# A windowed attention of a vision block on one core: per-query products and sums, and the same attention as matmuls over pairs of key rows

## The chip, the core and the metric

The kernel runs on one core of a Trainium2 chip. Five engines run their own queues of instructions and meet through semaphores: TensorE (PE in the profile; PEld are its weight loads), VectorE (DVE), ScalarE (ACT), GpSimd (POOL) and SyncE (SP), which here issues all DMAs. The metric is the device time of one execution in microseconds; lower is better.

## What is computed

The reference is a stack of layers on x of shape (2, 256, 56, 56) in float32. The change touches the first two of them, here cut to what matters. Group normalisation comes first, with groups of 8 channels; then attention over 7x7 windows with 8 heads of 32 channels, **without a softmax**; then a projection; then a position term from five values per pixel is added. `unfold` lists the 49 neighbours of each of the L = 50 x 50 window places; `attn_idx` gives every one of the 56 x 56 queries its window (the edge queries share the outermost ones).

```python
qkv = einsum('oc,bchw->bohw', qkv_w, x) + qkv_b
q = q * hd ** -0.5
def unfold(t):
    p = conv_general_dilated_patches(t, (7, 7), (1, 1), 'VALID')
    return p.reshape(B, C, L, 49)
k_u = unfold(k).reshape(B, nh, hd, L, 49).transpose(0, 1, 3, 2, 4)
k_g, v_g = k_u[:, :, attn_idx], v_u[:, :, attn_idx]
attn = einsum('bnld,bnldk->bnlk', qh, k_g) + bias
out = einsum('bnlk,bnlkd->bnld', attn, v_g)
x = x + einsum('oc,bchw->bohw', proj_w, out) + proj_b
```

The patches come out with the 49 taps ahead of the places, and `reshape(B, C, L, 49)` reads them as places ahead of taps. So the 49 keys of window place n are the elements 49 n to 49 n + 48 of the list "tap by tap, all places of a tap": nearly always a run of one tap over neighbouring pixels, that is pieces of one or two rows of the image. The rest of the reference (six state-space layers, a gated feed-forward layer, a causal attention, a mixture of eight experts) isn't touched.

## The kernel before

Three phases run one after the other: `conv_phase` (these two layers; it stores its result t1 to DRAM), `mamba_phase` and `tail_phase`. The order of instructions on each engine is the order of the Python calls; semaphores are set by the tile framework from the buffers that are read and written.

In `conv_phase` the 56 x 56 pixels are 7 chunks of 448 (CT). The channels are 2 x 128 partitions. `normalise` (L167 to L196) takes statistics with BatchNorm instructions (L172), sums them over the groups with a matmul (L177, L186), and scales x (L194). `project` (L199) makes q, k and v (L206 matmul, L216 ACT copy), kept as qo, kt, vt with channels on partitions.

The attention runs in 672 slots of 10, 10 or 8 queries: per image, 56 query rows of two halves of three slots each. For each half of a window row, `gather` (L294, copy L309 on ACT) puts the keys that the queries see into a row kr in the order of the queries, 49 per query, and the values likewise into vr; `edges` (L314, POOL) repeats the outermost window for the three edge queries. Then, slot by slot:

- `products` (L330, POOL, L335): key times query, elementwise, 128 partitions x 2 x 490;
- `sums` (L342, PE): the bias comes in as a matmul of a one-hot table with the bias table (L360), then a matmul with a block matrix of ones adds the 32 channels of a head and spreads the sum back to them (L368), both as 64x64 tiles at four positions of the array;
- `values` (L374, DVE): the score times the value, elementwise from PSUM (L377), and a sum over each 49 (L380), into qo.

The main loop (L443 on) calls products(i + 2), sums(i + 1), one step of `side_work` and values(i). `side_work` (L399) is a generator: the rest of the projections, the position term (`position`, L144; it goes to DRAM as pe_d, since the reference reads it with another shape), the second image's load and normalisation, and `output` (L228): it loads x and pe_d for a chunk (L231, L233), adds them on POOL (L236), multiplies by the projection (L244), adds on DVE (L253) and stores t1 (L261). Lines L461 on belong to mamba_phase: its first instructions are L487 (DVE), L490 (SP), L722 (SP, the load of t1's first chunk) and L727 (PE).

Of the kernel before, what the change touches and what calls it, by code (L numbers as in the profile page):

```python
# [18 lines left out]
P = 128  # L19
B = 2  # L20
# [9 lines left out]
OQ = 10  # L30
# [29 lines left out]

@with_exitstack
def conv_phase(ctx: ExitStack, tc: tile.TileContext, I, t1_d):


# [11 lines left out]
    HR = 25  # L76
    EDGE = 3 * KK
    HALF = HR * LW + EDGE
# [4 lines left out]
    rowp = ctx.enter_context(tc.tile_pool(name="cv_row", bufs=2))  # L83
    wp = ctx.enter_context(tc.tile_pool(name="cv_work", bufs=2))
    pmm = ctx.enter_context(tc.tile_pool(name="cv_pmm", bufs=2, space=PSUM))
    patt = ctx.enter_context(tc.tile_pool(name="cv_patt", bufs=3, space=PSUM))
# [7 lines left out]
    xg = big.tile([P, 2, S], F32, name="xg")  # L94
    kt = big.tile([P, 2, HW, HW], F32, name="kt")
    vt = big.tile([P, 2, HW, HW], F32, name="vt")
    qo = big.tile([P, 2, S], F32, name="qo")

    def load(b):
        for k in range(2):  # L100
            nc.sync.dma_start(xg[:, k, :], x_v[b, :, k, :])

    load(0)
    gmat = cp.tile([P, P], F32, name="gmat")
    nc.sync.dma_start(gmat, I["gmat"])
    wqkv = cp.tile([P, 2, 3 * C], F32, name="wqkv")
    nc.sync.dma_start(wqkv, I["qkv_wT"].rearrange("(k p) o -> p k o", p=P))
# [3 lines left out]
    rb = cp.tile([P, WS * 3 * 4], F32, name="rb")  # L111
    nc.sync.dma_start(rb, I["rel"])
    onehot = cp.tile([P, 3 * OQ * KK + 2 * (OQ - 2) * KK], F32, name="onehot")
    nc.sync.dma_start(onehot, I["onehot"])
    hmat = cp.tile([P, 2 * HD], F32, name="hmat")
    nc.sync.dma_start(hmat, I["hmat"])
    wproj = cp.tile([P, 2, C], F32, name="wproj")
    nc.sync.dma_start(wproj, I["proj_wT"].rearrange("(k p) o -> p k o", p=P))
    pew = cp.tile([5, C], F32, name="pew")
    nc.sync.dma_start(pew, I["pe_w"])  # L120
    eps = ones_column(nc, cp, 1e-5, "gn_eps")

    rel = cp.tile([P, WS, 3, 2, 2 * HD], F32, name="rel")
    nc.gpsimd.tensor_copy(
        rel.rearrange("j i c f (m d) -> j (i c f m) d", d=HD),
        rb.unsqueeze(2).to_broadcast([P, WS * 3 * 4, HD]),
    )

# [4 lines left out]
    def flow(groups):  # L133

        last = None
        for first, second in groups:
            first()
            if last:
                last()
            last = second  # L140
            yield
        last()

    def position(q):  # L144
        pos = wp.tile([5, CT], F32, name="pos", bufs=1)
        nc.sync.dma_start(pos, I["pos"][:, chunk(q, CT)])
        yield

        def group(i):
            pp = []  # L150

            def first():
                pp.append(mm())
                nc.tensor.matmul(
                    pp[0][:TK, :C], lhsT=pos[:, chunk(i, TK)], rhs=pew, start=True, stop=True
                )

            def second():
                pe = wp.tile([TK, C], F32, name="pe")
                nc.scalar.copy(pe, pp[0][:TK, :C])  # L160
                nc.sync.dma_start(pe_d[chunk(q * (CT // TK) + i, TK), :], pe)

            return first, second

        yield from flow(group(i) for i in range(CT // TK))

    def normalise():  # L167

        for k in range(2):
            st = wp.tile([P, NC, 6], F32, name="st")  # L170
            for j in range(NC):
                nc.vector.bn_stats(st[:, j, :], xg[:, k, chunk(j, CT)])  # L172
                yield
            mv = wp.tile([P, 2], F32, name="mv")
            nc.vector.bn_aggr(mv, st)
            pg = mm()
            nc.tensor.matmul(pg[:, 0:1], lhsT=gmat, rhs=mv[:, 0:1], start=True, stop=True)  # L177
            yield
            gm = wp.tile([P, 1], F32, name="gm")
            nc.vector.tensor_copy(gm, pg[:, 0:1])  # L180
            dm = wp.tile([P, 1], F32, name="dm")
            nc.vector.tensor_tensor(dm, mv[:, 0:1], gm, ALU.subtract)
            dv = wp.tile([P, 1], F32, name="dv")
            nc.vector.scalar_tensor_tensor(dv, dm, dm, mv[:, 1:2], ALU.mult, ALU.add)
            pv = mm()
            nc.tensor.matmul(pv[:, 0:1], lhsT=gmat, rhs=dv, start=True, stop=True)  # L186
            yield
            rs = wp.tile([P, 1], F32, name="rs")
            nc.scalar.activation(rs, pv[:, 0:1], AF.Sqrt, bias=eps)
            yield  # L190
            nc.vector.reciprocal(rs, rs)
            for j in range(NC):
                part = xg[:, k, chunk(j, CT)]
                nc.vector.tensor_scalar(part, part, gm, rs, ALU.subtract, ALU.mult)  # L194
                yield

    ready = set()

    def project(b, i, j, f):  # L199

        pq = []

        def first():
            pq.append(mm())
            for k in range(2):
                nc.tensor.matmul(  # L206
                    pq[0][:, :CT],
                    lhsT=wqkv[:, k, chunk(2 * i + f, P)],
                    rhs=xg[:, k, chunk(j, CT)],
                    start=(k == 0),  # L210
                    stop=(k == 1),
                )

        def second():
            dst = (qo, kt.rearrange("p f h w -> p f (h w)"), vt.rearrange("p f h w -> p f (h w)"))[i]
            nc.scalar.activation(  # L216
                dst[:, f, chunk(j, CT)], pq[0][:, :CT], AF.Identity,
                bias=vec[:, 2 * i + f : 2 * i + f + 1],
                scale=scale if i == 0 else 1.0,
            )  # L220
            ready.add((b, i, j, f))

        return first, second

    def parts(b, i, js):
        return [project(b, i, j, f) for j in js for f in range(2)]

    def output(b, j):  # L228

        xo = wp.tile([P, 2, CT], F32, name="xo", bufs=1)  # L230
        nc.sync.dma_start(xo, x_v[b, :, :, chunk(j, CT)])  # L231
        pe = wp.tile([P, 2, CT], F32, name="pe_in", bufs=1)
        nc.sync.dma_start(pe, pe_v[:, :, chunk(j, CT)])  # L233
        yield
        yield
        nc.gpsimd.tensor_tensor(xo, xo, pe, ALU.add)  # L236

        def group(f):
            po = []

            def first():
                po.append(mm())
                for k in range(2):
                    nc.tensor.matmul(  # L244
                        po[0][:, :CT],
                        lhsT=wproj[:, k, chunk(f, P)],
                        rhs=qo[:, k, chunk(j, CT)],
                        start=(k == 0),
                        stop=(k == 1),
                    )  # L250

            def second():
                nc.vector.scalar_tensor_tensor(  # L253
                    xo[:, f, :], po[0][:, :CT], vec[:, 6 + f : 7 + f], xo[:, f, :],
                    ALU.add, ALU.add,
                )

            return first, second

        yield from flow(group(f) for f in range(2))  # L260
        nc.sync.dma_start(t1_v[b, :, :, chunk(j, CT)], xo)  # L261

    halves, slots = [], []
    firsts = {}
    for b in range(B):
        for lh in range(LW):
            rows = [h for h in range(HW) if min(max(h - 3, 0), LW - 1) == lh]
            for e in range(2):  # L270
                n = len(halves)
                halves.append((b, lh, e, rows, len(slots)))
                for h in rows:
                    for w0, nq in ((0, OQ), (OQ, OQ), (2 * OQ, 8)):
                        slots.append((n, h, 28 * e + w0, nq))
        firsts[b + 1] = len(slots)
    ns = len(slots)
    K, V, PR, PA = {}, {}, {}, {}

    def pieces(n):

        b, lh, e, rows, _ = halves[n]
        a, z = (HR - 1) * e, (HR - 1) * e + HR
        found = []
        if a < lh:
            found.append((a, min(z, lh), *divmod(lh - 1, WS), LW - lh))
        if z > lh:  # L290
            found.append((max(a, lh), z, *divmod(lh, WS), -lh))
        return a, [(r0, r1, dw, dh + off) for r0, r1, dh, dw, off in found]

    def gather(n, which):  # L294
        if n >= len(halves):
            return
        b, lh, e, rows, _ = halves[n]
        a, found = pieces(n)
        for r0, r1, dw, of in found:
            for j in range((r0 + of) // CR, (r1 + of - 1) // CR + 1):  # L300
                for f in range(2):
                    while (b, 1 + which, j, f) not in ready:
                        next(work)
        t = rowp.tile([P, 2, HALF], F32, name=("kr", "vr")[which])
        (K, V)[which][n] = t
        at = 0 if e else EDGE
        m = t[:, :, at : at + HR * LW].rearrange("p f (r w) -> p f r w", w=LW)
# [1202 lines left out]
```

## Time and profile before

| what | us |
|---|---|
| runs of this kernel | 10,890.83, 10,893.99, 10,902.05 |
| their median | 10,893.99 |
| span of the profiled execution (its whole time is not listed beside it) | 10,877.0 |
| conv_phase, from the timeline: start to L261's last store | 0 to 1,668 |
| mamba_phase and tail_phase | 1,668 to 10,877 |
| busy over the span: PE / DVE / ACT / POOL | 8,985.9 / 9,661.4 / 7,670.7 / 8,265.3 |

How to read it: PE's busy time counts pipelined instructions, so 83% of the span is not PE at its peak. A row such as "L380 DVE TENSOR_REDUCE qo<-av 128x20 f32<-128x980 f32 x442 | 519.0, 1174 | 18.3 <-DVE av" says: line 380, on DVE, writes qo from av, 442 times, 519.0 us busy, 1,174 ns for one, and 18.3 us of idle time on the engine just before. The share over the whole span mixes three phases with different limits; for a change in the first one the stretches up to 1,668 us count.

### The profile page before, as it was taken

Reading aid. Unit: us, or ns where it says so; the run is one execution under the profiler, and the core shown is the slowest. Engines: PE = TensorE matmul, PEld = TensorE weight load, DVE = VectorE, ACT = ScalarE, POOL = GpSimd, SP = SyncE. Lnnn points to the kernel's source line nnn. Section 1 sums busy time; section 2 is a strip of 40 time slices with the busy share of each in tenths; the row PEclk is TensorE's granted clock in tenths of the full one; section 3 lists DMA queues with packets and bytes.
Section 4 is the critical chain, followed back from the end, with each engine's and each line's share of the span. In section 5 each row is a group of like instructions: output and inputs, shape, how many; then the busy total and the mean of one; then the engine's idle time right before and its main releaser. Section 6 shows DMA issues by size and latency. Waiting matters only on the chain. (4 is left out here: it accounts for less than half of the span.)

```text
span 10877.0 us, 121750 instructions
## 1 busy us (share of the span) xinstructions
PE 8985.9 (83%) x39394; PEld 3570.3 (33%) x39394; DVE 9661.4 (89%) x7545; ACT 7670.7 (71%) x15776; POOL 8265.3 (76%) x5268
## 2 busy tenths in 40 slices
PE   8999997777777777777777777777777777789999
PEld 3333333323322222222332222222222222245555
DVE  6998996999999999999999999999999999967453
ACT  4664665787777878778787777878787787733343
POOL 5887995788888888888888888888888888811100
PEclk9999998888888888888888888888888888799999
DMA  1000004555555555555555555555555555511111
GB/s 49 17 16 11 13 15 97 121 127 124 117 129 120 128 123 129 123 123 129 135 139 123 129 123 123 129 123 129 123 127 124 122 126 120 121 51 31 43 37 40
DMA packets 674228, 1068.88 MB, mean 98 GB/s; under 512 B 83082, under 2 KB 668050, under 8 KB 672722
## 3 DMA queue, kind: packets, MB, share of 16 engines
q1 hardware_dynamic: 673586, 1061.09, 42.0%
q8 instruction: 309, 5.06, 0.2%
q14 instruction: 333, 2.73, 0.1%
HBM read 875.91 MB, written 184.91 MB: 98 GB/s over the span
## 5 line engine op out<-in xcount | busy, mean ns | idle before, releaser
L824 POOL TENSOR_TENSOR x<-dtur,bc 128x896 f32<-128x896 f32 x2688 | 4701.9, 1771 | 109.8 <-PE acc L859 100.8
L807 ACT ACTIVATE da<-dtr,am 128x449 f32<-128x449 f32 x5376 | 3428.5, 638 | 187.8 <-DVE x L844 95.9
L844 DVE TENSOR_TENSOR_SCAN da<-da,x 128x898 f32<-128x898 f32 x1680 | 3397.5, 2022 | 150.2 <-ACT state L833 73.0
L837 POOL TENSOR_TENSOR x<-x,bc 128x896 f32<-128x896 f32 x1008 | 1788.5, 1774 | 513.3 <-ACT state L833 512.0
L562 PE MATMUL mm<-xn,w_in 128*128 128x448 f32 x2656 | 1481.2, 690 | 703.2 <-ACT hz L603 233.7
L844 DVE TENSOR_TENSOR_SCAN x<-da,x 128x898 f32<-128x898 f32 x1008 | 2002.3, 2013 | 0.7 <-ACT da L807 0.7
L837 DVE TENSOR_TENSOR x<-da,bc 128x896 f32<-128x896 f32 x1680 | 1834.5, 1092 | 82.4 <-DVE da L844 1.8
L859 PE MATMUL acc<-x,sum_w 128*32 128x448 f32 x10752 | 1565.5, 658 | 23.2 <-POOL x L837 17.3
L335 POOL TENSOR_TENSOR pr<-kr,qo 128x980 f32<-128x980 f32 (+1 forms) x672 | 1149.0, 1722 | 195.7 <-PE pa L368 185.5
L580 PE MATMUL mm<-u,w_cv 128*128 128x448 f32 x2656 | 1089.1, 553 | 175.3 <-ACT u L574 158.6
L562 PEld LDWEIGHTS mm<-xn,w_in 128*128 128x128 f32 x2656 | 549.8, 230 | 1675.2 <-issue 729.9
L833 ACT COPY state<-da 128x2 f32<-128x2 f32 x1680 | 264.0, 157 | 1058.3 <-DVE x L837 1043.6
L360 PE MATMUL pa<-onehot,rel 49*64 49x490 f32 (+5 forms) x7168 | 835.5, 558 | 111.9 <-DVE av L377 109.2
L377 DVE TENSOR_TENSOR av<-pa,vr 128x980 f32<-128x980 f32 (+1 forms) x672 | 740.2, 1102 | 113.3 <-PE pa L368 83.8
L380 DVE TENSOR_REDUCE qo<-av 128x20 f32<-128x980 f32 (+1 forms) x672 | 743.3, 1106 | 41.4 <-DVE av L377 1.0
L309 ACT COPY vr<-vt 128x2500 f32<-128x2500 f32 (+14 forms) x296 | 468.6, 1614 | 422.8 <-DVE av L377 422.5
L580 PEld LDWEIGHTS mm<-u,w_cv 128*128 128x128 f32 x2656 | 478.2, 190 | 800.0 <-issue 371.8
L652 POOL TENSOR_TENSOR dtu<-dt,hz 128x448 f32<-128x448 f32 x336 | 328.6, 978 | 450.8 <-ACT state L833 391.9
L368 PE MATMUL pa<-pr,hmat 64*64 64x490 f32 (+1 forms) x5376 | 643.4, 548 | 0.0
L708 PE MATMUL mm<-hz,w_out 128*128 128x448 f32 x1344 | 551.7, 554 | 79.5 <-DVE res L715 47.9
L633 PE MATMUL mm<-xd,w_dt 16*128 16x448 f32 x664 | 457.3, 777 | 189.9 <-ACT xd L620 110.9
L859 PEld LDWEIGHTS acc<-x,sum_w 128*32 128x32 f32 x10752 | 230.5, 117 | 1000.6 <-issue 790.4
(209 smaller groups left out, 11097.9 us busy)
## 6 DMA issues: line engine op xcount, KB each, us to landing
dtr<-dt_d SPq DMA_DIRECT2D x1344, 224.0 KB
dtur<-dtu_d SPq DMA_DIRECT2D x1344, 224.0 KB
bc<-bc_d SPq DMA_DIRECT2D x336, 448.0 KB
dt_d<-dt SPq DMA_DIRECT2D x336, 224.0 KB
dtu_d<-dtu SPq DMA_DIRECT2D x336, 224.0 KB
cb<-comb_d SPq DMA_DIRECT2D x128, 196.0 KB
t<-t_d SPq DMA_DIRECT2D x28, 448.0 KB
w_in<-in_in_w SPq DMA_DIRECT2D x12, 1024.0 KB
```

What stands on the lines that cost most here:

```text
L335: nc.gpsimd.tensor_tensor(pr[:, :, :m].rearrange("p f (q k) -> p f q k", k=KK), K[n][:, :, at : at + m].rearrange("p f (q k) -> p f q k", ...
L360: nc.tensor.matmul(pa[chunk(f, 64), g, :m], lhsT=rel[64 * g : 64 * g + rows, bh, kind, f, :], rhs=onehot[64 * g : 64 * g + rows, col : col ...
L368: nc.tensor.matmul(pa[chunk(f, 64), g, :m], lhsT=hmat[chunk(g, 64), :], rhs=pr[chunk(g, 64), f, :m], start=False, stop=True, tile_position ...
L377: nc.vector.tensor_tensor(av[:, :, :m], PA.pop(i)[:, :, :m], V[n][:, :, at : at + m], ALU.mult)
L380: nc.vector.tensor_reduce(qo[:, :, h * HW + w : h * HW + w + nq], av[:, :, :m].rearrange("p f (q k) -> p f q k", k=KK), AX.X, ALU.add,)
L562: nc.tensor.matmul(ps, lhsT=layer_of(j + 1)["w_in"][:, k, chunk(at, P)], rhs=Q["xn"][:, k, :], start=(k == 0), stop=(k == 1),)
L580: nc.tensor.matmul(ps, lhsT=layer_of(j + 1)["w_cv"][:, 4 * d + k, :], rhs=M["u", d][:, k : k + T], start=(k == 0), stop=(k == 3),)
L807: nc.scalar.activation(D[i][:, chunk(g, T + 1)], dtr[:, 2 * pr + g, :], AF.Exp, scale=L["am"][:, col : col + 1],)
L824: nc.gpsimd.tensor_tensor(x[:, :, 1:], Q[k][1][:, 2 * pr : 2 * pr + 2, :], wide(Q["bc"][:, ng, :]), ALU.mult)
L837: engine.tensor_tensor(both(X[i])[:, :, 1:], both(h)[:, :, 1:], wide(QS[j]["bc"][:, 4 + ng, :]), ALU.mult)
L844: nc.vector.tensor_tensor_scan(h, D[i], X[i], 0.0, ALU.mult, ALU.add)
L859: nc.tensor.matmul(acc[0][chunk(g, HD), :T], lhsT=sum_w, rhs=both(X[i - 1 + g // 2])[:, g % 2, 1:], start=False, stop=(ng == 3), tile_posi ...
```

## The change

`conv_phase` is written anew; only the loads of its inputs and `project`, `position`, `normalise` and `output` stay in kind. `mamba_phase` and `tail_phase` keep their code (their line numbers fall by 8).

The kernel now takes **two neighbouring rows of keys** (t - 1 and t, 112 pixels, KT) as one tile, for t = 0 to 55, and multiplies them with all the queries that use them. `key_plan` finds, at build time, for every query the tile in which its 49 keys lie, and a column s of that tile's 72 (QS). There are 48 queries whose keys are in two tiles; they get a second column and their two results are added. Everything of the attention is then matmuls with 112 keys on one side:

- `spread` copies the queries from image order (qn) into tile order (sk, 128 x 2 x 56 x 72, zero elsewhere), run by run, alternately on DVE and POOL (L274); `collect` copies the results back the same way, and adds the second columns on POOL (L297). Per image key_plan gives 228 runs and 48 second columns.
- `scores` (PE), for 7 tiles of one group and two heads: one matmul writes the bias of the inner queries (L356; a Toeplitz table `rel`, selected by a one-hot table); 14 small matmuls of key rows and queries add the scores (L365). The two heads are row tiles at different positions of the array.
- `weigh`: DVE multiplies with a mask (L375), which keeps of the 112 keys those that the query sees; POOL adds the bias of the 22 edge columns (L379).
- `value_part` (PE, L343): the values of the next group, pixels on partitions, straight from x; DVE adds their bias (L347).
- `apply` (PE, L391): 14 small matmuls of values and weighted scores; the two heads are column tiles. Every second call ACT copies the result back into sk (L398).
- `fetch` (L324 to L328) loads one-hot, mask and edge tables of the next group, 1.04 MB.

A unit is (group n, f, p): 8 groups, 4 head pairs, so 32 units per image; the order of calls is that of `attend`. Projections of all queries and keys, spread, collect and output are no longer beside the attention but before and after it; the second image's load and normalisation stay beside the first image's attention. `normalise` treats both channel halves together, `position` runs at the very start with pos lying in qn, and the x load is in smaller pieces. The tables are built on the host from the inputs, in another form than before (`layout`).

```diff
-OQ = 10
+QI = HW - 6
+QS = HW + 16
+QE = QS - QI
...
+def window(v):
+    return min(max(v - WS // 2, 0), LW - 1)
+def key_plan():
+    used, found = set(), []
+    def take(tile, h, main):
+        s = h - 3 if 3 <= h < HW - 3 else QI + (h if h < 3 else h - (HW - 6))
+        if not main or (tile, s) in used:
+            s = HW
+            while (tile, s) in used:
+                s += 1
+        assert s < QS
+        used.add((tile, s))
+        return s
+    for h in range(HW):
+        for w in sorted(range(HW), key=lambda w: not 3 <= w < HW - 3):
+            lh, lw = window(h), window(w)
+            parts = {}
+            for k in range(KK):
+                tap, place = divmod((lh * LW + lw) * KK + k, LW * LW)
+                row, col = place // LW + tap // WS, place % LW + tap % WS
+                parts.setdefault((row, tap), []).append((k, col))
+            keys = [(row, tap, p) for (row, tap), p in parts.items()]
+            main, last = 3 <= w < HW - 3, lh == lw == LW - 1
+            if lh != lw:
+                row = lw - lh + (lh // WS if lw > lh else LW + (lh - 1) // WS)
+                found.append((row, take(row, h, main), h, w, keys))
+                continue
+            for row, tap, p in keys:
+                tile = row if tap == lh or last else (row + 1) % HW
+                found.append((tile, take(tile, h, main and not last), h, w, [(row, tap, p)]))
+    return found
...
     CT = 448
-    HR = 25
-    EDGE = 3 * KK
-    HALF = HR * LW + EDGE
+    KT = 2 * HW
+    GT = 7
+    NG = HW // GT
+    GS = GT * QS
...
-    rowp = ctx.enter_context(tc.tile_pool(name="cv_row", bufs=2))
+    twop = ctx.enter_context(tc.tile_pool(name="cv_two", bufs=2))
-    patt = ctx.enter_context(tc.tile_pool(name="cv_patt", bufs=3, space=PSUM))
+    psc = ctx.enter_context(tc.tile_pool(name="cv_psc", bufs=2, space=PSUM))
+    pout = ctx.enter_context(tc.tile_pool(name="cv_pout", bufs=2, space=PSUM))
...
+    nc.gpsimd.memset(sk, 0.0)
...
+    def move(pairs):
+        for to, of in pairs:
+            (nc.vector.tensor_copy, nc.gpsimd.tensor_copy)[turn[0] % 2](to, of)
+            turn[0] += 1
+    def places(h):
+        for w, n, at, step in runs[h]:
+            yield (
+                qn[:, :, h * HW + w : h * HW + w + n],
+                flat[:, :, at : at + (n - 1) * step + 1 : step],
+            )
+    def spread(j):
+        for h in range(j * CR, (j + 1) * CR):
+            move((s, q) for q, s in places(h))
+            for h2, w, t, s in seconds:
+                if h2 == h:
+                    move([(sk[:, :, t, s : s + 1], qn[:, :, h * HW + w : h * HW + w + 1])])
+    def collect(j):
+        for h in range(j * CR, (j + 1) * CR):
+            move(places(h))
+        for h, w, t, s in seconds:
+            if h // CR == j:
+                q = qn[:, :, h * HW + w : h * HW + w + 1]
+                nc.gpsimd.tensor_tensor(q, q, sk[:, :, t, s : s + 1], ALU.add)
     def output(b, j):
-        xo = wp.tile([P, 2, CT], F32, name="xo", bufs=1)
+        xo = wp.tile([P, 2, CT], F32, name="xo")
         nc.sync.dma_start(xo, x_v[b, :, :, chunk(j, CT)])
         pe = wp.tile([P, 2, CT], F32, name="pe_in", bufs=1)
         nc.sync.dma_start(pe, pe_v[:, :, chunk(j, CT)])
...
+    def fetch(n):
+        if n >= B * NG:
+            return
+        g = n % NG
+        oh = twop.tile([P, GS], F32, name="oh")
+        nc.sync.dma_start(oh, I["onehot"][g])
+        mk = twop.tile([KT, GS], F32, name="mk")
+        nc.sync.dma_start(mk, I["mask"][g])
+        bm = twop.tile([KT, 4, 2, GT, QE], F32, name="bm")
+        nc.sync.dma_start(bm, I["edge"][g])
+        tables[n] = oh, mk, bm
+    def value_part(n, i):
+        b, g = divmod(n, NG)
+        if b >= B:
+            return
+        if i == 0:
+            values[n] = twop.tile([KT, GT, C], F32, name="vt")
+        m = min(2, GT - 2 * i)
+        ps = mm()[:KT].rearrange("p (n c) -> p n c", n=2)
+        for r in range(m):
+            at = (g * GT + 2 * i + r) * HW
+            for k in range(2):
+                nc.tensor.matmul(
+                    ps[:, r, :], lhsT=xg[b][:, k, at : at + KT], rhs=wqkv[:, k, 2 * C :],
+                    start=(k == 0), stop=(k == 1),
+                )
+        nc.vector.tensor_tensor(
+            values[n][:, 2 * i : 2 * i + m, :], ps[:, :m, :], vb[:, :m, :], ALU.add
+        )
+    def scores(n, f, p):
+        b, g = divmod(n, NG)
+        oh = tables[n][0]
+        ps = psc.tile([P, 2, 512], F32, name="ps")
+        for i in range(2):
+            nc.tensor.matmul(
+                ps[:KT, i, :GS], lhsT=rel[64 * i : 64 * i + HW, 2 * f + p, :],
+                rhs=oh[64 * i : 64 * i + HW, :], start=True, stop=False,
+                tile_position=(64 * i, 0),
+            )
+        for r in range(GT):
+            t = g * GT + r
+            for i in range(2):
+                hd = chunk(p + 2 * i, HD)
+                nc.tensor.matmul(
+                    ps[:KT, i, chunk(r, QS)], lhsT=kt[hd, f, t * HW : t * HW + KT],
+                    rhs=sk[hd, f, t, :], start=False, stop=(r == GT - 1),
+                    tile_position=(HD * (p + 2 * i), 0),
+                )
+        scored[n, f, p] = ps
+    def weigh(n, f, p):
+        _, mk, bm = tables[n]
+        at = wp.tile([KT, 2, GS], F32, name="at", bufs=3)
+        nc.vector.tensor_tensor(
+            at, scored[n, f, p][:KT, :, :GS], mk.unsqueeze(1).to_broadcast([KT, 2, GS]), ALU.mult
+        )
+        edge = at.rearrange("j i (r s) -> j i r s", s=QS)[:, :, :, QI:]
+        nc.gpsimd.tensor_tensor(edge, edge, bm[:, 2 * f + p], ALU.add)
+        scored[n, f, p] = at
+    def apply(n, f, p):
+        g = n % NG
+        at = scored.pop((n, f, p))
+        if p == 0:
+            outs[n, f] = pout.tile([P, 512], F32, name="po")
+        po = outs[n, f]
+        for r in range(GT):
+            for i in range(2):
+                hd = p + 2 * i
+                nc.tensor.matmul(
+                    po[chunk(hd, HD), chunk(r, QS)],
+                    lhsT=values[n][:, r, f * P + hd * HD : f * P + (hd + 1) * HD],
+                    rhs=at[:, i, chunk(r, QS)], start=True, stop=True,
+                    tile_position=(0, HD * hd),
+                )
+        if p == 1:
+            nc.scalar.copy(
+                sk[:, f, g * GT : (g + 1) * GT, :],
+                outs.pop((n, f))[:, :GS].rearrange("p (t s) -> p t s", s=QS),
+            )
+    def attend(b, side):
+        units = [(n, f, p) for n in range(b * NG, (b + 1) * NG) for f in range(2) for p in range(2)]
+        scores(*units[0])
+        for u, (n, f, p) in enumerate(units):
+            if u % 4 == 0:
+                fetch(n + 1)
+            weigh(n, f, p)
+            if u + 1 < len(units):
+                scores(*units[u + 1])
+            if n + 1 < (b + 1) * NG:
+                value_part(n + 1, 2 * f + p)
+            for _ in range(2):
+                next(side, None)
+            apply(n, f, p)
+        for _ in side:
+            pass
+    position()
+    for _ in normalise(0):
+        pass
+    fetch(0)
+    for j in range(NC):
+        for f in range(2):
+            project(0, 0, j, f)
+        spread(j)
+    keys(0)
+    for i in range(4):
+        value_part(0, i)
+    attend(0, later())
+    keys(1)
+    for i in range(4):
+        value_part(NG, i)
+    for j in range(NC):
+        collect(j)
+        output(0, j)
+    for j in range(NC):
+        for f in range(2):
+            project(1, 0, j, f)
+        spread(j)
+    attend(1, iter(()))
+    for j in range(NC):
+        collect(j)
+        output(1, j)
```

## The prediction, on record before the run

> **What bounds the kernel now.** I read the table of busy time by stretch first, because the change touches only conv_phase and the page's averages run over all three phases. (Columns: stretch, its length, then busy us and count on PE, PEld, DVE, ACT, POOL; granted clock; DMA share; GB/s.)
>
> ```profile
> 400.00:800.00 400.00, 371.69 (x3388) 125.35 (x3384) 384.72 (x366) 277.27 (x186) 357.15 (x301) 1.00 0.05 15
> ...
> 1500.00:1600.00 100.00, 91.53 (x852) 30.09 (x848) 97.50 (x94) 68.81 (x45) 91.14 (x78) 1.00 0.05 15
> ```
>
> DVE is busy 96 to 98% of the attention, POOL 89 to 91%, DMA 5%. Second, the groups up to 1640 us, shapes apart, say with what:
>
> ```profile
> L335 POOL TENSOR_TENSOR pr<-kr,qo 128x980 f32<-128x980 f32 x445 | 807.8, 1833 | 161.3 <-PE pa L368 151.2 <-DVE dv L184 1.3 <-DVE qo L380 0.5
> L380 DVE TENSOR_REDUCE qo<-av 128x20 f32<-128x980 f32 x442 | 519.0, 1174 | 18.3 <-DVE av L377 0.5
> L377 DVE TENSOR_TENSOR av<-pa,vr 128x980 f32<-128x980 f32 x442 | 517.0, 1170 | 98.0 <-PE pa L368 68.5 <-POOL vr L321 29.3
> ```
>
> With the 784-wide forms (213 each) DVE spends some 1,470 us on L377 and L380. Third, the waits of 100 to 1650 us name what PE waits for: DVE again, 471 us of them.
>
> ```profile
> PEld pa L360 <- DVE av L377: 471.4, 515, 7.3
> ```
>
> Fourth, the timeline at the border shows the end of the phase:
>
> ```profile
> 1668.09 0.36 SPq L261 DMA_DIRECT2D t_d<-xo  x1
> 1668.12 0.17 DVE L487 MEMSET mb_mean_w<- 128x128 f32 x1
> ...
> 1669.61 0.47 SPq L722 DMA_DIRECT2D t<-t_d  x1
> ...
> 1673.36 3.32 PE L727 MATMUL da<-t,mb_mean_w 128*128 128x448 f32 x4 [6.06 <-DMA t<-t_d]
> ```
>
> The second phase starts when the last chunk is stored: nothing hides conv_phase. It takes 1,668 us, and the other 10,877.0 - 1,668 = 9,209 us keep their code. So the sum is a new length for conv_phase. The runs' median, 10,893.99, lies 17 us above the profiled span; I add the 17 at the end.
>
> **Units of price on PE.** A matmul in the code is two instructions in the trace (L360: 3,584 issued, 7,168 shown). Two bursts at full clock give the step of tiny matmuls, set by their weight load:
>
> ```profile
> 1729.10 1.65 PEld L666 LDWEIGHTS da<-mb_mean_w,sq 128*112 128x112 f32 x16 [2.28 <-ACT sq L662]
> 1729.10 1.73 PE L666 MATMUL da<-mb_mean_w,sq 128*112 128x1 f32 x16 [1.56 <-ACT sq L662]
> ...
> 9983.36 1.47 PE L1154 MATMUL pl<-wrt,x 128*98 128x8 f32 x16
> ```
>
> Less the 0.23 to 0.25 that one takes, 15 steps are 1.48 and 1.24 us: 0.098 for 112 weight columns, 0.083 for 98, or 0.87 ns a column. L206's loads in the timeline (28.51, 28.88, 29.26) are 0.375 apart for 448 moving columns: 0.84 ns a column. The price of an instruction is the larger of the two, since loads run beside matmuls: L612, whose loads have 48 columns instead of 128, has the same step (8 in 3.2 us, (3.2 - 0.54) / 7 = 0.38). And tiles at different positions run together:
>
> ```profile
> 1491.57 1.00 PE L368 MATMUL pa<-pr,hmat 64*64 64x490 f32 x8
> 1491.57 0.15 PEld L368 LDWEIGHTS pa<-pr,hmat 64*64 64x64 f32 x4 [0.26 <-issue]
> ```
>
> Eight instructions in two steps of 0.41, four loads in 0.15. A change of tile shape costs about 0.1:
>
> ```profile
> 1559.69 0.59 PE L368 MATMUL pa<-pr,hmat 64*64 64x490 f32 x4
> 1560.21 0.30 PEld L244 LDWEIGHTS mm<-qo,wproj 128*128 128x128 f32 x2 [0.78 <-issue]
> ```
>
> L368's step of 0.41 ends at 1560.10; the full-array L244, which waits for nobody, begins at 1560.21.
>
> **What goes.** All of L335, L360, L368, L377, L380, L309 and L321, that is the DVE-bound 1,600 us, for 2 images.
>
> **The unit that replaces it.** (L274 to L398 are lines of the changed code, as the diff numbers them.) 64 units (8 groups, f, p, 2 images), on PE in the order scores(u+1), value_part, apply(u):
> - bias: 2 matmuls of 504 columns in two row tiles, beside each other: first load 0.09 + 2 x 0.42 = 0.93;
> - scores: 14 matmuls, 112 weight columns, 72 moving, alternating between two row tiles: first load 0.10 + 7 x 2 x 0.098 = 1.47;
> - value_part: 4 matmuls of 256 columns (2 in one unit of four): first load 0.11 + 8 x 0.215 = 1.83, on average 1.62;
> - apply: 14 matmuls, 32 weight columns, 72 moving, two column tiles: 0.03 + 14 x 0.065 = 0.94;
> - four changes of shape: 0.4;
> - two waits on PE's own semaphore (L356, L343) drain it: 0.25 each (one short matmul, L1190: 247 ns), 0.5.
>
> Sum 5.86 us; in an image's last group, without value_part, 4.1. An image: 28 x 5.86 + 4 x 4.1 = 180; both 361 us. Unknown is whether 32-row tiles overlap as the 64x64 ones do. Below: all overlaps and no drains, 329. Above: the two tiles one after the other (bias 1.77, scores 2.84, apply 1.85, values and changes as above, no drains, 8.5), 530. I stay near the lower end: the nearest rows (L368; L859 with four 128*32 tiles) overlap.
>
> Does another engine end later? DVE per unit: weigh, 1008 wide from PSUM, 1.2 (L377); the value add 0.67 (L715, 448 wide, 0.605); beside image 0 two steps of normalise, 1.2 (L172 0.61). The chain value_part(u) - add 0.67 - side 1.2 - weigh(u+1) 1.2 - POOL edge 308 wide 0.7 (L335 scaled plus 0.16) - apply(u+1), with hand-overs 4.0, lies beside apply(u), scores and bias(u+2) and value_part(u+1), some 5.4. Hidden, with 1.4 us to spare; if that cover went, the excess is paid 28 times. ACT: one copy of 0.58 in two units. fetch: 1.04 MB a group, issued four units (22 us) early, at the 400 GB/s of the first loads 2.6 us: hidden.
>
> **Around the units.** Moves: key_plan gives 228 runs and 48 second parts an image, so spread issues 276 copies, half on DVE, half on POOL; collect 228 plus 48 POOL adds. Small ones on DVE take 0.16 (L180, 128x1) plus 0.03, on POOL 0.2 (between L538's 0.11 and L110's 0.24); elements add 3 us. Spread: 28 us DVE, 31 POOL. Collect: DVE 24; POOL 114 x 0.2 + 48 x 0.24 + 3 = 37.
> - Start, 93 us: position's 14 steps hang on two pe buffers, each held by copy 0.6, issue 0.4 and a store of about 2.3 us, 1.7 a step behind the first loads, to about 38; normalise's first matmul is queued behind it on PE; then 42.5 the first Q, Q and K 21 us each (28 matmuls x 0.75), values 6. Spread ends near 80, beside K.
> - Between the images, 121 us: keys(1) and values 27 on PE, and DVE's collect stands behind the value adds; then seven chunks, each a ring, since pe_in has one buffer and SP issues the next loads behind the store: stt 1.4, three issues 1.3, loads 3 (L722 to L727 above 3.7; SP's wait for t_d, 29.4 us over 13, 2.3), POOL add 2.1 (L236), hand-overs 0.4: 8.2 to 8.8 us, in all 60; then Q and spread(1), 34.
> - End, 60: the same ring, with nothing beside it.
> - Filling and draining the unit pipe, 5 an image.
>
> Sum 93 + 121 + 60 + 10 + 361 = 645 us; 9,209 + 645 = 9,854; **9,871 us** with the 17, call it 9,870: faster by 9.4%.
>
> **The rivals.**
> 1. *Small tiles don't overlap, or can't be fed* (0.25). With tiles in series, 530 instead of 361: 10,040. If PE can't be fed faster than its densest stretch in this trace (L666, 0.098 a pair; 67.5 pairs a unit = 6.6), 28 x 6.6 + 4 x 5.9 per image: 417, 9,928. If a load waits for matmuls on the same rows, a step is the sum: scores 14 x 0.163, values 8 x 0.31, apply 14 x 0.092, so 7.8 us and 480: 9,990. For it: no row shows 32-row tiles. Against: L206, L612, L859.
> The Trainium skill (TensorE: Matmul & The Clock Gate, Part 3: Packing small matmuls — row/col tiling) states this last one: a weight load overlaps matmuls in flight only where the row group differs. By that rule the time would be that 9,990; the trace (L206 and L612 with one step of 0.375 to 0.38) disagrees for full-array matmuls.
> 2. *Moves and rings are the bound* (0.12): a strided two-element copy at the 0.43 of L321's row. Spread and collect then cost some 30 us more each, four times, half of it covered in the start, and rings at the half clock that L244 shows at 1661 to 1667 (0.75 a step) 10.5 instead of 8.5: about 100 us more, 9,970. The slow copies must come in the gaps between attends to count.
> 3. *Slower than before* (0.02): every small matmul pays its whole latency instead of a step. Place: scores and apply, 56 instructions a unit. Price: L177's 334 ns gives 18.7, with bias and values 21.6 us a unit. It decides from (1,668 - 284) / 64 = 21.6 on, so from about 0.34 us an instruction; at L177's 0.334 it stands at the break-even, at 0.44 (L682's mean) 27.6 us a unit: 11,280. Against: L666 and L1154 pipeline.
>
> **Numbers.** The forecast's own case (0.58) runs from 9,790 (329 us of units, rings 8) to 9,950; 0.03 is for what I don't see. The range goes to rival 1's serial tiles with part of rival 2: 9,790 to 10,070. About 0.2% is what a measurement of this kernel tells from no change. Faster 0.97, same 0.01, slower 0.02.
>
> **What would show it.** Right: conv_phase ends near 640 us; in attend PE is the busy engine at clock 1.0, a unit every 5.3 to 6.2 us, and DVE about 40 to 60% busy. Units of 8 us with pairs of L365 in series: rival 1. L274 in the gaps at 0.3 us and more: rival 2. The forecast fails above all if the gaps are not the 274 us that I put together from rings and copies, or if DVE's value add is late for weigh, so that PE waits for POOL before L391.

## The result, and the profile after

The changed kernel takes 9,833.06 us, median of four runs (9,825.32 to 9,847.44), against 10,895.06 for the kernel before (10,890.83 to 10,902.05): a ratio of 0.9024, 95% interval 0.9011 to 0.9037. The forecast was 9,870, the range 9,790 to 10,070. The profiled execution took 9,833.15, 1.85 us more than its span.

The border of the phases in the timeline:

```profile
609.62 0.36 SPq L315 DMA_DIRECT2D t_d<-xo  x1
609.65 0.17 DVE L479 MEMSET mb_mean_w<- 128x128 f32 x1
```

conv_phase ends at 609.6 us instead of 1,668; 645 was forecast. The table of busy time by stretch (columns as before):

```profile
200.00:250.00 50.00, 50.00 (x641) 36.07 (x641) 16.92 (x21) 2.90 (x5) 7.03 (x9) 1.00 0.16 48
...
400.00:450.00 50.00, 50.00 (x648) 36.18 (x646) 16.04 (x19) 2.90 (x5) 7.07 (x10) 1.00 0.21 59
550.00:600.00 50.00, 28.89 (x44) 12.22 (x42) 17.29 (x96) 0.00 (x0) 31.63 (x131) 0.75 0.41 138
```

In the attention the engines have changed places: PE fills all of the 50 us, DVE 16 to 17 (32 to 34%, it was 96 to 98), POOL 7. The last row is the end ring: no engine is busy two thirds of the time, and the clock is 0.75. The groups between 60 and 760 us, by shape, show the new costs:

```profile
L343 PE MATMUL mm<-wqkv,xg 128*112 128x256 f32 x448 | 114.5, 399 | 0.0
L365 PE MATMUL ps<-sk,kt 32*112 32x72 f32 x1792 | 105.0, 265 | 1.1 <-DVE sk L274 1.1
...
L375 DVE TENSOR_TENSOR at<-ps,mk 112x1008 f32<-112x1008 f32 x64 | 76.6, 1197 | 17.2 <-PE ps L365 17.2
...
L391 PE MATMUL po<-at,vt 112*32 112x72 f32 x1792 | 69.8, 230 | 2.5 <-POOL at L379 2.5
```

L365's 1,792 matmuls are busy 105 us in all, though a single one lasts 265 ns, which would be 475 us: they run in a pipe, two tiles beside each other. The idle time at the end of the rows is the other half of the reading: in both images PE waited 2.5 us for POOL's L379, where its weight loads had waited 471 us for DVE before. What follows is one full unit in the timeline, with PE's rows, L391's weight loads and the neighbours:

```profile
444.28 1.20 DVE L375 TENSOR_TENSOR at<-ps,mk 112x1008 f32<-112x1008 f32 x1
...
444.83 1.10 PE L356 MATMUL ps<-oh,rel 56*112 56x504 f32 x4
...
445.61 0.78 POOL L379 TENSOR_TENSOR at<-at,bm 112x308 f32<-112x308 f32 x1 [3.55 <-PE po L391]
...
445.86 1.60 PE L365 MATMUL ps<-sk,kt 32*112 32x72 f32 x28
...
447.39 1.98 PE L343 MATMUL mm<-wqkv,xg 128*112 128x256 f32 x8
...
449.30 0.89 PEld L391 LDWEIGHTS po<-at,vt 112*32 112x32 f32 x28 [0.34 <-issue]
449.30 1.07 PE L391 MATMUL po<-at,vt 112*32 112x72 f32 x28
449.41 0.69 DVE L347 TENSOR_TENSOR vt<-mm,vb 112x512 f32<-112x512 f32 x1 [3.93 <-PE mm L343]
...
450.30 1.10 PE L356 MATMUL ps<-oh,rel 56*112 56x504 f32 x4
```

Read from start to start: bias 1.03, scores 1.53, values 1.91, apply 1.00, together 5.47. POOL's edge ends at 446.39, and L391, which needs it, begins at 449.30: 2.9 us to spare.

Two things were not in the forecast. In image 0, PE waits 1.39 us for DVE before normalise's L204, and from 138.44 on everything on PE takes nearly twice as long:

```profile
136.93 0.58 PE L204 MATMUL mm<-mv,gmat 128*128 128x1 f32 x4 [1.39 <-DVE mv L201]
...
138.44 2.02 PE L356 MATMUL ps<-oh,rel 56*112 56x504 f32 x4
...
140.39 2.89 PE L365 MATMUL ps<-sk,kt 32*112 32x72 f32 x28
```

The granted clock was 0.5 from 138.5 to 159.0. And the end ring takes 9.4 us a chunk:

```profile
562.34 0.36 SPq L315 DMA_DIRECT2D t_d<-xo  x1
562.79 0.42 SPq L301 DMA_DIRECT2D xo<-in_x  x1
563.31 0.68 SPq L303 DMA_DIRECT2D pe_in<-pe_d  x1
...
568.39 2.07 POOL L304 TENSOR_TENSOR xo<-xo,pe_in 128x896 f32<-128x896 f32 x1 [3.24 <-issue]
...
571.83 0.36 SPq L315 DMA_DIRECT2D t_d<-xo  x1
```

The loads are issued behind the store, and L304 begins 4.4 us after the second issue ended.

### The profile page after: what moved, and what is told of

Same layout as the page of the kernel before. It is cut to its first block, busy times and chain, and to the rows that moved or that the text cites. A ratio compares the mean times of both kernels' runs of the same rounds, so it can differ in the third digit from the quotient of the medians.

```text
span 9831.3 us, 102094 instructions
## 1 busy us (share of the span) xinstructions
PE 7995.7 (81%) x31026; PEld 3378.5 (34%) x31026; DVE 8388.8 (85%) x6835; ACT 6758.1 (69%) x15177; POOL 7120.1 (72%) x4860
## 5 line engine op out<-in xcount | busy, mean ns | idle before, releaser
L700 PE MATMUL mm<-hz,w_out 128*128 128x448 f32 x1344 | 552.0, 554 | 80.2 <-DVE res L707 47.8
L815 ACT COPY x<-state 128x2 f32<-128x2 f32 x2688 | 521.7, 194 | 0.0
L1348 DVE TENSOR_TENSOR hid<-hid,cb 128x784 f32<-128x784 f32 x128 | 135.2, 1057 | 423.8 <-ACT hid L1345 400.4
L658 PE MATMUL mm<-mb_mean_w,sq 128*112 128x1 f32 x1744 | 259.5, 279 | 231.0 <-ACT sq L654 230.2
L846 PE MATMUL acc<-hz,w_sk 128*128 128x448 f32 x672 | 369.4, 635 | 63.1 <-DVE hz L861 61.8
L700 PEld LDWEIGHTS mm<-hz,w_out 128*128 128x128 f32 x1344 | 242.5, 190 | 403.7 <-issue 191.2
```

What stands on the lines that cost most here:

```text
L700: nc.tensor.matmul(ps, lhsT=layer_of(j - 1)["w_out"][:, d, chunk(k, P)], rhs=QS[j - 1]["hz"][:, d, :], start=(d == 0), stop=(d == NB - 1),)
L815: nc.scalar.copy(x[:, :, 0:1], states(i))
L846: nc.tensor.matmul(acc[0][:, :T], lhsT=L["w_sk"][:, k, :], rhs=Q["hz"][:, k, :], start=True, stop=False,)
```

## The experiments

Each starts from the changed kernel; the code shown is cut, with `...` for what is left out. The phases behind conv_phase have the same code in all of them, and yet they took 9,204 to 9,267 us in the profiled executions. So the length of conv_phase in the trace is the measure, and the whole time is given beside it; where no range stands with it, it is a single execution. "Half clock" is the sum of the records with a granted clock of 0.5 inside the two attentions.

**Tiles in series** (e1_serial): in L365's and L391's loops the head is the outer loop.

```diff
-        for r in range(GT):
-            for i in range(2):
+        for i in range(2):
+            for r in range(GT):
```

> scores (L365) and apply (L391) issue all seven matmuls of the first head and then all seven of the second, instead of alternating; same instructions, same output. My theory (tiles at different positions run beside each other, which two neighbours in the queue need): L365 takes near 2.8 us instead of 1.6 and L391 near 1.85 instead of 1.07, a unit 7.3 to 7.7 us instead of 5.47, the first phase some 110 to 135 us longer (about 730 us), the whole about 9,950. Rival (the alternation does nothing: a small matmul simply costs less than its columns say): unit 5.47, whole 9,833.

Measured: 9,960.11; conv_phase 754.1. In a full unit:

```profile
571.72 2.63 PE L365 MATMUL ps<-sk,kt 32*112 32x72 f32 x28
...
575.33 1.72 PE L391 MATMUL po<-at,vt 112*32 112x72 f32 x28
```

L365 takes 2.63 us instead of 1.60 and L391 1.72 instead of 1.07; a unit takes 7.16 at full clock. So the overlap is real and hangs on the order in the queue: the same instructions without alternation cost 1.69 us a unit more. The phase grew by more than expected, 144.5 us; 2 x 32 units by 1.69 are 108. The rest is in the clock column, and PE was not even idle there:

```profile
480.00:680.00 200.00, 200.00 (x1799) 157.34 (x1796) 45.67 (x52) 8.11 (x14) 21.65 (x28) 0.91 0.13 36
```

Half clock 58.0 and 47.8 us, against 20.5 and about 1 in the changed kernel.

**Four times weigh on DVE** (e2_weigh4).

```diff
-        nc.vector.tensor_tensor(
...
+        for _ in range(4):
+            nc.vector.tensor_tensor(
...
```

> weigh's product (L375, 1.20 us on DVE) is issued four times, with the same result, so 3.6 us more of DVE work a unit. My theory (DVE lies beside PE with 2.9 us to spare in image 1, read from the row of L379 that ends at 446.39 and the row of L391 that begins at 449.30): the unit grows by the excess alone, 0.6 to 0.9 us, to 6.1 to 6.4; beside normalise in image 0 by 1.9 or so; the whole 60 to 90 us longer, about 9,905. Rival (DVE is in series with PE, as it was before the change): unit 9.1, the whole 230 us longer, 10,060. Rival (DVE doesn't matter at all): 5.47, 9,833.

Measured: 9,943.38; conv_phase 722.6, 113 longer, where 60 to 90 were expected. In image 1 (no side work) a unit is 1.55 us longer on average, (213.8 - 164.3) / 32. The timeline of the unit in which the cover runs out (L376 and L392 are L375 and L391):

```profile
520.39 0.78 POOL L380 TENSOR_TENSOR at<-at,bm 112x308 f32<-112x308 f32 x1 [5.87 <-DVE at L376]
...
521.23 1.07 PE L392 MATMUL po<-at,vt 112*32 112x72 f32 x28 [1.97 <-POOL at L380]
...
523.61 2.89 PE L365 MATMUL ps<-sk,kt 32*112 32x72 f32 x28
```

PE waits 1.97 us for POOL's edge, late behind DVE, and then runs at half clock: L365 takes 2.89. In image 1 PE waits 26.4 us at L392 in all, 0.83 a unit, near the excess of 0.7 (3.6 us of work less 2.9 to spare). Half clock was 54.2 us of image 1; work done at half speed there costs up to 27 us more, 0.85 a unit. The two together come to a little over the 1.55, so the split is not exact. Both rivals, serial and "doesn't matter", fall, the slack is about as read, and an excess is paid about twice, once as a wait and once through the clock.

**Apply twice** (e3_apply2).

```diff
-        for r in range(GT):
+        for r in [*range(GT), *range(GT)]:
```

> apply's 14 matmuls (L391) are issued twice, with the same result. My theory (PE's terms add up, one for one): the unit grows by 14 steps of 0.065 to 0.07, so by 0.9 to 1.0 us, from 5.47 to 6.4, the whole 58 to 64 us longer, about 9,895. Rival (a wait sets the unit, PE has room in it): under 0.3 us a unit, the whole under 20 us longer.

Measured: 9,872.37; conv_phase 663.5, 53.9 longer; a full unit 6.34, so 0.87 more: 14 steps of 0.062. PE's terms add one for one. The whole grew by only 39 because the phases behind came out at 9,207 instead of 9,222.

**No wait in normalise** (e4_nowait).

```diff
             nc.vector.bn_aggr(mv[k], st[k])
+        yield
+        yield
         pg = mm()
...
-            nc.tensor.matmul(pv[:, k : k + 1], lhsT=gmat, rhs=dv, start=True, stop=True)
+            dvs.append(dv)
+        yield
+        yield
+        pv = mm()
+        for k in range(2):
+            nc.tensor.matmul(pv[:, k : k + 1], lhsT=gmat, rhs=dvs[k], start=True, stop=True)
```

> In normalise, both small matmuls with gmat (L204, L216) are issued one unit later than what they read on DVE, so that PE does not stand 1.39 us before them; nothing else is changed. My theory (that wait is what took the granted clock to 0.5 from 138.5 to 159.0 us in the first attention): no half clock inside attend, its units stay at 5.47, and the first phase ends 10 to 13 us earlier, near 598. Rival (the clock falls by itself, or for the data or power drawn there): the half-clock stretch stays, near 610; the whole 9,833 within 5.

Measured: 9,822.81; conv_phase 601.9. The stretch from 130 to 165 us, first of the changed kernel, then of this one:

```profile
130.00:165.00 35.00, 32.22 (x289) 22.75 (x289) 9.84 (x20) 1.57 (x4) 3.12 (x4) 0.71 0.11 31
```

```profile
130.00:165.00 35.00, 35.00 (x461) 25.81 (x458) 15.56 (x29) 2.15 (x5) 5.27 (x7) 1.00 0.20 54
```

The half clock is gone from the first attention, which takes 163.1 us instead of 175.3. So two waits of PE of 1.39 us each (L204, L216) cost 12 us here. That is no fixed price: the same two waits, as long, stand in other runs, and the half clock behind them was 20.5 us in e7 and e10 too, but 13.7 in e5, 10.2 in e6 and 6.8 in e3. The phase gained 7.7, not 10 to 13: a piece of half clock fell at the start of the second attention instead (371.4 to 378.3, one unit 8.7), some 2.7 us, and the time between the attentions was 2.7 longer.

**Loads ahead** (e5_loads; inputs holds output's two loads, and pe_in gets two buffers) and **loads and copies ahead** (e6_both, with collect(j + 1) in the place of collect(j)).

```diff
+    first = inputs(0, 0)
...
     for j in range(NC):
+        then = inputs(0, j + 1)
         collect(j)
-        output(0, j)
+        output(0, j, first)
+        first = then
```

> pe_in gets two buffers and the loads of chunk j+1 (xo, pe_in) are issued before the store of chunk j; the first pair before keys(1) and before the second attention. In the changed kernel a chunk of collect and output takes 9.4 us (L315 at 562.34, 571.83, 581.19), of which the loads behind the store take 5. My theory has two loops that share this ring: store - loads - L304 - L312 - store (9.4), and, once the loads are early, L312 - DVE's copies of the next chunk, queued behind it (2.0) - L308 (5.0 at the mixed clock) - hand-overs 0.4 - L312 (1.3), 8.7. So a chunk falls only to 8.4 to 8.8, and the first phase ends 8 to 14 us earlier than 609.6, near 598. Rival (the loads alone are the ring): a chunk falls to POOL's own work, 2.07 + 2.9 + 1.3 = 6.3, and the phase ends near 570. Rival (the ring is bound elsewhere, loads are hidden): 9.4 and 610.

> As the run before, and collect(j+1) is issued ahead of output(j), so that the copies of the next chunk no longer stand behind L312 on DVE. Two loops (my theory): both are cut, a chunk falls to POOL's own work, 2.07 for L304, 2.9 for its copies, 1.3 for its adds, so 6.3 to 6.7; the first phase ends near 570 (14 chunks by 2.9, 41 us off 609.6). If loads alone are the ring: the same as the run before. If PE at half clock is the bound, a chunk is 5 to 5.5 plus hand-overs.

Measured: e5 9,813.67, conv_phase 584.8, 24.8 shorter, between what I expected (8 to 14) and what the rival of loads alone gives (40); e6 9,838.99, conv_phase 569.7 (its phases behind took 9,267, the longest of all). In e5's end ring the stores are 7.4, 6.0, 7.8, 5.7, 7.9 and 9.2 us apart (540.76 to 584.81), 7.3 on average where it was 9.4: less than my 8.4 to 8.8, since up to 567 L308 ran at half clock in every second chunk only (3.27 and 4.7), and only the second L312, 0.68, stands in that loop. POOL still waits 0.99 for DVE's copies ahead of its adds, so that loop exists. In e6 it is cut, and a chunk is what POOL has to do:

```profile
548.99 2.06 POOL L310 TENSOR_TENSOR xo<-xo,pe_in 128x896 f32<-128x896 f32 x1
...
551.00 3.15 POOL L274 COPY qn<-sk 128x6 f32<-128x6 f32 x18
...
554.11 1.25 POOL L297 TENSOR_TENSOR qn<-qn,sk 128x2 f32<-128x2 f32 x8
555.31 2.06 POOL L310 TENSOR_TENSOR xo<-xo,pe_in 128x896 f32<-128x896 f32 x1
```

6.3 us from add to add with no idle time; 569.7 was expected as 570. So the ring of the changed kernel was the loads behind the store first (24.8 us of the phase), and DVE's copies behind L312 as soon as the loads were early (another 15.1).

**Residual beside the attention** (e7_early), and the same **without normalise's wait** (e8_all).

```diff
+    def refill(b, j):
+        part = slice(HW + j * CT, HW + (j + 1) * CT)
+        nc.sync.dma_start(xg[b][:, :, part], x_v[b, :, :, chunk(j, CT)])
+        nc.sync.dma_start(qn[:, :, chunk(j, CT)], pe_v[:, :, chunk(j, CT)])
...
+    def residual(b, j):
+        part = xg[b][:, :, HW + j * CT : HW + (j + 1) * CT]
+        nc.gpsimd.tensor_tensor(part, part, qn[:, :, chunk(j, CT)], ALU.add)
...
             if u % 4 == 0:
                 fetch(n + 1)
+                if u:
+                    refill(b, u // 4 - 1)
             weigh(n, f, p)
+            if u % 4 == 3 and u > 4:
+                residual(b, u // 4 - 1)
```

> x and the position term are loaded and added during the attention, one chunk a group, into rows of xg and qn that are free by then; the seven L304 adds an image (2.07 us each on POOL) move beside the units; collect(0..6) of image 0 is issued before keys(1), and in the last image one chunk ahead of output. Theory (PE sets the unit and POOL has 4.7 us to spare in it; the rings are made of loads, adds and copies): units stay at 5.47, the end falls from 67 to 36 to 45 us (POOL's copies and adds 4.3 a chunk, PE 3 to 5), the time between the attentions from 111 to 78 to 90, the first phase ends at 548 to 562, the whole near 9,778. Rival (the adds and loads moved into the attention delay L379 or collide with fetch, and the clock falls in the waits): units of 6.5 to 7.5 wherever an add stands, the attentions 10 to 20 us longer, half of the gain gone.

> The run before with normalise's two small matmuls issued one unit later as well (the run without that wait took the half clock out of the first attention and ended the first phase at 601.9 instead of 609.6). If the gains add: the first phase ends 8 to 12 us earlier than in the run before, near 545; the whole 9,760 to 9,772, 0.6 to 0.75% below the changed kernel. Rival (the clock falls in other places instead, since the governor averages): no gain over the run before.

Measured: e7 9,750.73, conv_phase 533.8; units stay at 5.47 outside the half clock behind normalise's waits, and the phase is shorter than the expected 548 to 562: 69.8 us between the attentions (110.6 before), 33.6 at the end (67.5). The moved adds show in POOL's column, and PE's stays full:

```profile
400.00:450.00 50.00, 50.00 (x642) 36.19 (x640) 15.55 (x19) 2.89 (x5) 13.67 (x13) 1.00 0.39 114
```

e8: conv_phase 523.9, 9.9 less, so the gains add; median of five runs 9,766.12 (9,749.36 to 9,781.38), ratio to the kernel before 0.8952, interval 0.8936 to 0.8967.

**Both once more on one chip** (e10_again is the changed kernel, e11_best is e8).

> The changed kernel itself once more, to stand on one chip beside the next. Expected: 9,825 to 9,850, 0.900 to 0.904 of the kernel before; conv_phase 605 to 612.

> The version with both early residuals and no wait in normalise, once more, on the same chip as the changed kernel. If its first phase is 86 us shorter (523.9 against 609.6) and the rest is the same code, the medians lie 60 to 95 us apart, 0.6 to 1.0%; if the gain is lost in the phases behind, under 30.

Measured: 9,834.33 (9,824.87 to 9,841.52), ratio 0.9023, interval 0.9008 to 0.9039; and 9,772.33 (9,764.56 to 9,776.98), ratio 0.8966, interval 0.8951 to 0.8980. conv_phase 610.2 and 523.6. The best version is 62 us faster, 0.6%, of 86.6 us won in its phase. The other 25, by the medians, are lost behind it. In the profiled executions the later phases took 9,213 us after the changed kernel and 9,252 after this one (e8 9,256, e7 9,215), from 2 less to 10 more in each of the second phase's twelve passes. Part of those 39 is the spread between executions of one kernel: five of e8 lie 32 us apart. What does the rest stays open.

**What brings the clock down** (e9_fill: serial, with twice the value matmuls; e12_split: serial, the value matmuls in two halves between the small ones).

> As the serial run (no alternation in L365 and L391), and value_part's full-array matmuls (L343) are issued twice with the same result, some 1.8 us more PE work in a unit with values (9.0 us instead of 7.16). In the serial run the granted clock was 0.5 in 58.0 of 244 us and 47.8 of 239 us of the two attentions, though PE was busy all the time. Theory (the granted clock follows how much of the array is in use, and 32-row or 32-column tiles alone leave most of it empty): with more full-array work in each unit the half clock nearly goes, under 15 us in each attention apart from normalise's wait. Rival (it follows time or the number of instructions): 20% of the attentions again, 55 to 65 us in each. First phase 850 to 870 us by the theory, 890 and more by the rival.

> As the serial run, the same instructions, but the value matmuls of a unit (L343, full array) are issued in two halves, one between the bias and the scores, one after the scores, instead of all after the scores. In the serial run apply, bias and scores (small tiles) follow on each other for 1.72 + 1.10 + 2.63 = 5.45 us, and the clock was 0.5 in 58 and 48 us of the two attentions; with twice the full-array work elsewhere in the unit it was 68 and 82. Theory (the granted clock is decided over stretches of about 3.4 us, the shortest in its records, and falls when small tiles fill one): no stretch of small tiles is longer than 2.8 us now, a unit is 7.2 to 7.4, and the half clock falls under 20 us in each attention, normalise's wait included; first phase 710 to 725. Rival (it falls for the load or the heat of the whole unit, wherever its parts stand): 45 to 60 us again, first phase 750 to 765.

Measured: e9 10,096.58, conv_phase 877.0, half clock 68.3 of 294 us and 81.9 of 298. More full-array work does not bring the clock back: that theory falls. e12 9,980.29, conv_phase 760.7, half clock 61.4 and 34.1 us, where under 20 was expected: that one falls too, and the phase is even 6.6 us longer than e1's (a unit at full clock takes 7.34, not 7.16). In 200 us of units of image 1 the half clock was 34.1 in e1 (480 to 680), 42.8 in e9 (545 to 745) and 17.1 in e12 (488 to 688); over whole attentions e12 has less than e1 only in image 1 (34.1 for 47.8) and more in image 0 (61.4 for 58.0). With one execution of each, it is not shown that parting the small tiles helps. That the order of the same work has a part in it is shown by e1 against the changed kernel: the same instructions, 47.8 us of half clock in image 1 against about 1. By what rule stays open.

## Why the prediction was right

- **The mechanism**: right. conv_phase alone changed, DVE stopped being the bound, and PE with its units became it.
- **The units**: right in kind, 11% high. Four terms without changes of shape were put at 5.17 us in a full unit, and the whole unit measured 5.47; if the terms are right, the changes cost 0.3 in all, not 0.4. The **two drains of 0.5** are not there: PE's rows show no wait before L356 or L343, and the 0.3 leaves no room for them. The average unit of a group is (3 x 5.47 + 4.61) / 4 = 5.26 against 5.86, the last group's 3.56 against 4.1, the fill of the pipe some 3 us an image against 5. Both attentions: 164.3 in image 1, 175.3 in image 0, where the half clock took the 12 us back that e4 returned; together 339.6 against 371, the largest miss.
- **Overlap of the small tiles** (rival 1): shown by the rows and by e1. The fed rate is no bound either: L391's 28 loads take 0.89 us with their matmuls beside them, 0.032 a pair, a third of rival 1's 0.098. And no load waited for matmuls on the same rows: value_part's full-array units took 1.91 to the next start, not the 2.5 of 8 x 0.31. The Trainium skill's rule (TensorE: Matmul & The Clock Gate, Part 3: Packing small matmuls — row/col tiling), by which a load overlaps only where the row group differs, would have made the unit 7.8; the trace disagrees with 5.47. The same section, in its account of the mechanism, also lets a load go ahead when it goes to a background weight buffer; the trace does not contradict that wider wording, and no run here shows the buffer.
- **The chain over DVE and POOL**: hidden, as said, and with more room: 2.9 us in image 1, where the prediction's terms without side work give 1.4 + 1.2 = 2.6. What an excess costs was put too low: e2 shows it paid again through the clock. DVE's share, forecast at 40 to 60%, was 32 to 34%, and 47% only beside normalise (23.29 of the 50 us from 100 to 150); I had read the side work into both images.
- **Start**: 93 against 92 (the parts that it names add up to 90.5). **Between the images**: 121 against 110.6. Keys and values took 27.4 us (267.39 to 294.8; 27 forecast) and the rings 62 (60), but from Q's first matmul at 356.55 to the first unit it was 21 and not 34: the copies of spread(1) run beside Q, chunk by chunk. **End**: 60 against 67.5; the ring's term "loads 3" is 4.4 measured, and 8.2 to 8.8 became 9.4. These two errors nearly cancel, by luck.
- **Moves** (rival 2): L274's copies take 192 to 216 ns on DVE and 201 to 212 on POOL at 2 to 8 elements, against 0.19 and 0.20: right, and far from 0.43. Of rival 2 the half clock in the rings came true, in about half of the time (0.75 and 0.76 in their stretches).
- **The rest**: 9,209 against 9,221.7, and the 17 us above the span were 1.85. These two are mostly one error that cancels itself: in every execution listed the time lies 1.7 to 2.9 us above the span, so the span of 10,877.0 came from an execution some 15 us faster than the median, and 9,209 is low by about what the 17 is high. The sum of the misses: -1.1 - 31.4 - 10.4 + 7.5 + 12.7 - 15.2 = -37.9, from 9,871 to 9,833; the units are the one large miss.
- **The range**: its lower end is not what its terms give. With 329 us of units and rings of 8 it is 9,871 - 32 - 8 = 9,831, not 9,790. The measured 9,833 lies at that end of the forecast's own case, that of all overlaps and no drains.

## What to carry over

As far as this kernel shows: price a stream of small matmuls by its step, from the densest burst of the same engine, not by the duration of one; add a tenth of a microsecond or less for each change of shape, and nothing for a wait that was satisfied before its turn. Let tiles at different positions alternate in the queue: the same instructions one position after the other cost some 60% more (2.63 for 1.60, 1.72 for 1.07). After a change that takes the bound away, read the gaps between the new stages with the same care: here loads behind a store, copies and adds that could be done earlier and two short waits on PE were worth 86 us of 610.

## What had not been expected of the hardware

- A wait of PE of 1.39 us was followed by 20.5 us at a granted clock of 0.5, and issuing the waiting matmuls a unit later (e4, and again e8 and e11) took that away: 12 us for 1.4, or 2.8 with the wait before L216 inside that stretch. In e3, e5 and e6 the same two waits were followed by 6.8 to 13.7. In image 1 of e2, from 450 to 610 us, each of the five waits of 1.96 or 1.97 us was followed by half clock (3.4 to 10.2 us), and none of the seven of 0.9 to 1.1. The clock's records are 3.4 us or multiples of it long.
- The clock also fell with PE busy without a gap (200.00 of 200.00 us, clock 0.91 in e1), when small tiles stood one after the other; twice the full-array work (0.89 in 200 us of e9) didn't cure it, and it isn't shown that parting the small ones by it does (0.96 in 200 us of e12, but no less half clock in its first image). The cause is open.
- Unchanged code behind conv_phase took 9,204 to 9,267 us in the profiled executions, a spread larger than what e3, e4, e5 and e6 each changed in conv_phase. Executions of one and the same kernel differ by 32 us (e8) and 41 us (the kernel before, nine of them, 10,882.64 to 10,923.37), so how much of the spread hangs on the kernel is open.
